# Transposing normalised rows through the vector engine and DRAM instead of the tensor engine, in one fused transformer block

## The chip, the cores and the metric

The kernel runs on one core of a Trainium2 chip. A core has five engines with queues of their own: PE (TensorE, matmuls), DVE (VectorE), ACT (ScalarE), POOL (GpSimd) and SP (SyncE, which here only issues DMAs). Each engine works its queue strictly in order, and engines wait for each other by semaphores. The metric is device time in microseconds (us), the median of several executions.

## What is computed

One pre-norm transformer block in float32, for 4 inputs ("batches", B) of 512 rows (T) by 512 columns (D). Cut to what matters:

```python
x = x + attn(layernorm(x))        # x: (4, 512, 512)
x = x + ffn(layernorm(x))

def attn(n):                      # 32 query heads, 8 key/value heads, 16 wide
    q, k, v = n @ Wq, n @ Wk, n @ Wv
    q, k = rope(q), rope(k)
    p = softmax(causal(q @ k.T / 4))
    return (p @ v) @ Wo

def ffn(n):                       # hidden width 1376
    return (silu(n @ Wg.T) * (n @ Wu.T)) @ Wd.T
```

PE contracts over the partition axis, so each `layernorm(x) @ W` needs the normalised rows transposed: columns of x on the 128 partitions. There are eight such operands of 512 x 512: one ahead of the projections and one ahead of the ffn, for each of 4 inputs.

## The kernel before

Rows are worked in NT = 4 tiles of 128 rows. For one tile, `statistics` (L179) takes mean and variance on DVE and the power of -0.5 on POOL, and `normalised` (L189) writes the normalised rows on DVE. `transposed` (L211) then transposes the tile on PE: four `nc.tensor.transpose` of 128 x 128 against the identity (L214) into one PSUM bank, which ACT (L219) or, for odd tiles outside the first slot, DVE (L217) copies into `xnT`, an SBUF tile of 128 x (4 x 512).

Attention is done in 32 groups, 8 for each input; one group is four heads of one input. `slot(b, steps)` (L673) runs the eight groups of input b by hand in program order. A group has four "visits" (scores on PE at L456 and L461, the row maximum on DVE at L479, the exponential on ACT at L529, the causal mask on POOL at L533), a last visit, and the product with the values (L555). PE work of other stages is handed to a slot as a list of (cost, step) and is spread evenly over it: after each of the 4 visits, `gap()` issues the next steps until the sum of their costs has reached its 32nd part of the whole list. This filling is what keeps PE busy. The lists:

- slot 0 (attention of input 0): projections of inputs 1 (rest), 2 and 3. `projections(b)` gives `begin` (loads of the rows, and statistics and normalisation pushed on a queue), `turned` (the four transposes) and `rest` (24 steps: keys, first queries, values, three more queries, 4 steps each).
- slot 1 (attention of input 1): what is left of input 3's projections, the output product `attended(0)` of input 0 (8 steps, L354) with its normalisation and transposes (`behind`), `hidden(0)` (gate and up products, 44 steps, L399) and half of `down(0)` (20 steps in all, L424).
- slots 2 and 3: the rest of the previous input's `down`, woven with `attended` by `woven` (L722), then `hidden`, then the first half of `down`.
- after slot 3 there is no attention left: the rest of `down` of input 2, then `attended`, `hidden` and `down` of input 3.

DVE work that isn't urgent waits in Python queues. `aside` holds statistics, normalisations and the spread of keys; `full` holds what has to be done with a finished PSUM bank in slot 0; `later` holds the reciprocals of the softmax sums. After each visit, `odd_steps(us)` (L201) takes steps from these queues by their stated costs until a budget of 1.4 to 1.9 is used, so that this work is placed on DVE between one visit's maxima and the next's. Outside slot 0, `fill` also does up to two `aside` steps after each PE step.

The keys' `finish` (L282) rotates the projected keys (DVE shuffle L248, POOL product L249, DVE product L250, POOL sum L251) into `kr` and puts `spread` at the head of `aside`: a DVE shuffle of `kr` (L288) and four POOL products (L290).

A row minimum for each group takes a path through DRAM: `turned_round` (L516, a DVE transpose in 32 x 32 squares, and its store L517) and `laid_out` (L526, four small loads into the next-but-one group's queries). All these DMAs, the loads of rows (L176, L272), of ffn weights (`load_f`, L160) and the stores of results (L429) are issued on SP in program order.

Gate and up weights go through `shared`, three places of 1024 columns; its first two hold Wq and its third Wk and Wv until the projections are done. `load_f(c)` fills place c % 3. `xnTs[""]` is the operand of inputs 0, 2 and 3 and of every ffn; input 1 uses part of `wd_sb`.

The order of slot 1 is, in full:

```python
slot(1, [before[0], *rest3[-12:-4], *before[1:], *rest3[-4:], firsts, *behind,
         *layer[:4], after(spilled), *layer[4:20], after(load_down), *layer[20:], *tiles[:cut]])
```

## Time and profile before

The time is 944.59 us (median of 3 runs, 943.49 to 946.97). The profile shows one execution, whose own time was 946.11 us and whose span (first to last recorded instruction) is 944.4 us.

| | busy us | share of the span | instructions |
|---|---|---|---|
| PE, matmul | 908.7 | 96% | 4672 |
| PE, weight load (beside the matmuls) | 406.3 | 43% | 4672 |
| DVE | 511.8 | 54% | 1514 |
| ACT | 225.0 | 24% | 295 |
| POOL | 216.6 | 23% | 324 |
| DMA, queue of SP | 15.1% of 16 engines | | 64160 packets |

The group boundaries can be read from the first score matmul of each group: slot 0 runs from 60.3 to 204.9 us, slots 1 to 3 from there to about 792 us, and the rest is the tail. Busy time is a share of a stage; where PE is busy without gaps, only less PE work makes the stage shorter, and where it has gaps, what ends the gaps counts.

### The profile page before, as it was taken

What the parts mean: (1) busy time and instruction counts of PE and PEld (TensorE: products, weight loads), DVE (VectorE), ACT (ScalarE), POOL (GpSimd) and SP (SyncE); (2) the same over time, 40 slices, a digit from 0 to 9 for tenths busy, and PEclk for the clock granted to TensorE, in tenths of its full rate; (3) what the DMA queues carried; (4) which work ended last, traced back from release to release, by engine and by line L of the source; (5) the groups of instructions that cost most, each with busy time, mean ns of one, the idle gap of its engine ahead of it and who ended that gap; (6) DMA issues with size and microseconds to landing.
All of it is one profiled execution on the core that took longest, in us unless ns stands there. A gap on an engine that the chain in (4) does not pass through costs nothing.

```text
span 944.4 us, 12662 instructions
## 1 busy us (share of the span) xinstructions
PE 908.7 (96%) x4672; PEld 406.3 (43%) x4672; DVE 511.8 (54%) x1514; ACT 225.0 (24%) x295; POOL 216.6 (23%) x324
## 2 busy tenths in 40 slices
PE   6889889989999999999999999999999999999998
PEld 3444444444444444444444444444444444444443
DVE  7667777767755555565646463666465512422200
ACT  1013333331323232222232322223232321001000
POOL 4554354544221212122111111221111111100000
PEclk9999899999999999999999999999999999999999
DMA  6010100000421610130221110101121011032100
GB/s 222 2 47 2 47 3 2 3 2 2 160 83 41 188 41 24 47 146 12 57 69 45 41 47 13 57 12 47 48 56 46 19 45 67 12 97 72 37 12 33
DMA packets 64510, 47.42 MB, mean 50 GB/s; under 512 B 13536, under 2 KB 56544, under 8 KB 64192
## 3 DMA queue, kind: packets, MB, share of 16 engines
q1 hardware_dynamic: 64160, 40.84, 15.1%
q10 hardware_dynamic: 288, 5.77, 1.6%
q8 instruction: 37, 0.61, 0.3%
q14 instruction: 25, 0.20, 0.1%
HBM read 39.00 MB, written 7.60 MB: 49 GB/s over the span
## 4 chain that ended last, share of the span: by engine, by line
PE 80%; DVE 9%; POOL 5%; issue 2%; ACT 2%; DMA 0%; POOLq 0%; SPq 0%; DVEq 0%; ACTq 0%
PE mm L399 33%; PE mm L424 17%; PE sc L456 13%; PE mm L354 6%; PE sc L461 5%; DVE junk L479 5%; PE mm L240 4%; POOL qa L444 2%; ACT e L529 2%; POOL e L533 1%; PE mm L214 1%; PE av L555 1%; DVE st L183 1%; POOL rot L249 1%; PE mm L303 1%
## 5 line engine op out<-in xcount | busy, mean ns | idle before, releaser
L479 DVE CUSTOM_DVE_ANT_0 junk<-sc,mask 128x128 f32<-128x128 f32 (+3 forms) x512 | 251.1, 490 | 178.0 <-PE sc L461 94.3
L399 PE MATMUL mm<-xnT,shared 128*128 128x512 f32 (+1 forms) x704 | 317.5, 600 | 0.0
L529 ACT ACTIVATE e<-sc 128x1024 f32<-128x1024 f32 (+1 forms) x192 | 165.4, 881 | 477.4 <-PE sc L461 382.5
L399 PEld LDWEIGHTS mm<-xnT,shared 128*128 128x128 f32 (+1 forms) x704 | 127.4, 187 | 166.9 <-issue 161.7
L533 POOL TENSOR_SCALAR_AFFINE_SELECT e<-e 128x512 f32<-128x512 f32 (+1 forms) x160 | 85.2, 543 | 411.9 <-ACT e L529 394.3
L456 PE MATMUL sc<-home,qa 32*128 32x512 f32 (+3 forms) x1024 | 164.7, 464 | 15.3 <-DVE low L479 13.1
L461 PE MATMUL sc<-qa,home 32*128 32x512 f32 (+3 forms) x1024 | 165.9, 472 | 0.5 <-DVE low L479 0.3
L424 PE MATMUL mm<-wd_sb,home 128*128 128x512 f32 (+1 forms) x352 | 158.4, 599 | 0.0
L456 PEld LDWEIGHTS sc<-home,qa 32*128 32x128 f32 x1024 | 76.2, 189 | 116.8 <-issue 30.5
L424 PEld LDWEIGHTS mm<-wd_sb,home 128*128 128x128 f32 (+1 forms) x352 | 64.8, 190 | 83.9 <-issue 82.4
L461 PEld LDWEIGHTS sc<-qa,home 32*128 32x128 f32 x1024 | 72.6, 186 | 26.7 <-issue 14.4
L555 PE MATMUL av<-e,home 128*32 128x512 f32 (+3 forms) x1024 | 78.1, 437 | 0.8 <-POOL e L533 0.7
L408 DVE SCALAR_TENSOR_TENSOR g<-g,mm 128x512 f32<-128x512 f32 (+1 forms) x44 | 29.8, 678 | 81.3 <-ACT g L407 81.3
L240 PE MATMUL mm<-xnT,shared 128*128 128x512 f32 x120 | 62.4, 651 | 1.5 <-issue 0.8
L410 DVE TENSOR_TENSOR home<-mm,g 128x512 f32<-128x512 f32 (+1 forms) x44 | 30.2, 685 | 55.4 <-PE mm L399 55.0
L581 DVE RECIPROCAL inv<-inv 128x128 f32<-128x128 f32 x64 | 58.0, 932 | 0.5
L354 PE MATMUL mm<-wo_sb,cx 128*128 128x512 f32 x128 | 58.1, 600 | 0.0
L407 ACT ACTIVATE g<-mm 128x512 f32<-128x512 f32 (+1 forms) x44 | 26.3, 597 | 116.0 <-PE mm L399 116.0
L555 PEld LDWEIGHTS av<-e,home 128*32 128x32 f32 x1024 | 29.9, 109 | 44.2 <-issue 40.0
L428 DVE SCALAR_TENSOR_TENSOR xr<-mm,xr 128x512 f32<-128x512 f32 x16 | 10.9, 683 | 68.2 <-PE mm L424 68.2
L479 DVE DVE_READ_ACCUMULATOR2_ANT low<- 128x1 f32 x512 | 42.5, 83 | 0.0
L186 POOL TENSOR_TENSOR rstd<-rstd,neghalf 128x1 f32<-128x1 f32 x32 | 21.5, 673 | 73.1 <-DVE rstd L185 73.1
(66 smaller groups left out, 439.0 us busy)
## 6 DMA issues: line engine op xcount, KB each, us to landing
shared<-in_wg SPq DMA_DIRECT2D x40, 256.0 KB
shared<-in_wu SPq DMA_DIRECT2D x40, 256.0 KB
xr<-in_x SPq DMA_DIRECT2D x16, 256.0 KB
out<-xr SPq DMA_DIRECT2D x16, 256.0 KB
xa<-in_x SPq DMA_DIRECT2D x12, 256.0 KB
spill<-wd_sb ACTq DMA_DIRECT2D x1, 2816.0 KB
home<-spill ACTq DMA_DIRECT2D x1, 2816.0 KB
wd_sb<-in_wd SPq DMA_DIRECT2D x1, 2560.0 KB
```

What stands on the lines that cost most here:

```text
L240: nc.tensor.matmul(ps, lhsT=w[:, k, ts(m, P)], rhs=xnT[:, k, :], start=k == 0, stop=k == NK - 1)
L354: nc.tensor.matmul(ps, lhsT=cx[m][:, ts(i, P)], rhs=wo_sb[:, m, :], start=m == 0, stop=m == 3)
L399: nc.tensor.matmul(ps[:m, :], lhsT=wgu[c][:, a, k, :m], rhs=xnTs[""][:, k, :], start=k == 0, stop=k == NK - 1)
L410: nc.vector.tensor_tensor(homes[n][:m, f, :], ps[:m, :], gs[f][:m, :], ALU.mult)
L424: nc.tensor.matmul(py[i], lhsT=homes[n][:m, f, ts(i, P)], rhs=wd_sb[:m, f, :], start=f == 0, stop=f == NF - 1)
L456: nc.tensor.matmul(dst, lhsT=qa[g][rows_of(r), ts(i, P)], rhs=k, start=True, stop=True)
L461: nc.tensor.matmul(dst, lhsT=k, rhs=qa[g][rows_of(r), P * j :], start=True, stop=True)
L479: nc.vector.tensor_tensor_reduce(out=junk[:, :n], in0=src, in1=mask[:, T - n :], scale=-1.0, scalar=BIG, op0=ALU.add, op1=ALU.min, accum_o ...
L529: nc.scalar.activation(dst, src, AF.Exp, scale=1.0 / math.sqrt(DH))
L533: nc.gpsimd.affine_select(out=e[:, heads, c : c + P], in_=e[:, heads, c : c + P], compare_op=ALU.is_ge, fill=0.0, base=0, pattern=[[0, hea ...
L555: nc.tensor.matmul(av[32 * r : 32 * r + 32, P * j :], lhsT=v[:, j, 4 * (m // 2) + r, DH * (1 - hf) : DH * (3 - hf)], rhs=e[:, r, c : c + n ...
L581: nc.vector.reciprocal(r[:, ts(n, P)], r[:, ts(n, P)])
```

## The change

Six of the eight operands (the projections of inputs 2 and 3 and all four of the ffn) are no longer transposed on PE. A new function transposes a normalised tile on DVE in 32 x 32 squares, stores it square by square to its transposed place in a DRAM buffer `flip`, and loads finished column blocks back as `xnT`. Inputs 0 and 1 keep the path over PE. The costs stated for a normalisation in the queue become 1.2 in place of 0.6, those of `turned` and `behind` become 0. Input 3 gets an operand buffer of its own. `spread` of the keys goes to a new queue `soon`, and reaches `aside` at the second `odd_steps` after it. Four steps (input 3's values) move from slot 0 to slot 1, four steps of `down(2)` from slot 3 to the tail, and in `woven` the first four other steps come ahead of `before[0]`. The places of the ffn weights are rotated by two, and the second of the first two weight loads is issued after the last projection step.

```diff
-    xnTs = {"": const.tile([P, NK, T], F32, name="xnT")}
-    xnTs[1] = homes[3][:, :NK, :]
+    xnTs = [const.tile([P, NK, T], F32, name=f"xnT{n}") for n in range(2)]
+    xnT_of = {0: xnTs[0], 1: homes[3][:, :NK, :], 2: xnTs[0], 3: xnTs[1]}
+    flip = [dram.tile([D, T], F32, name=f"flip{n}") for n in range(2)]
...
     def odd_steps(us, banks=True):
+        for n in range(len(soon)):
+            left, step = soon.popleft()
+            if left > 0:
+                soon.append((left - 1, step))
+            else:
+                aside.appendleft(step)
...
+    def flipped(xn, i, n, dst):
+        t = work.tile([P, D], F32, tag="g", name="xt", bufs=2)
+        nc.vector.transpose(t, xn)
+        turned = flip[n].rearrange("(c d) (i r s) -> i r d c s", d=32, r=4, s=32)
+        for r in range(4):
+            rows = t[32 * r : 32 * r + 32, :]
+            nc.sync.dma_start(out=turned[i, r], in_=rows.rearrange("d (c s) -> d c s", s=32))
+        for a in [i - 1, i] if i == NT - 1 else [i - 1] if i > 0 else []:
+            nc.sync.dma_start(out=dst[:, :, ts(a, P)], in_=flip[n].rearrange("(k p) t -> p k t", p=P)[:, :, ts(a, P)])
...
     def norm(i):                                   # in projections
         normalised(xn[i], found[i])
+            if b > 1:
+                flipped(xn[i], i, b % 2, xnT)
...
-                    aside.appendleft((0.75, spread))
+                    soon.append((1, (0.75, spread)))
...
     def norm(i):                                   # in attended
         normalised(xn[i], found[i])
+            flipped(xn[i], i, b % 2, xnTs[0])
...
-        def tail(i):
-            while i not in xn:
+        def tail():
+            while NT - 1 not in xn:
                 do(aside)
-            transposed(xn[i], i, xnTs[""])
...
-        t = shared[:, c % 3, :, :, :]
+        t = shared[:, (c + 2) % 3, :, :, :]
...
-        return [before[0], *others[:4], *before[1:], *others[4:-1], *behind, others[-1]]
+        return [*others[:4], *before, *others[4:-1], *behind, others[-1]]
...
-    slot(0, [begin2, *rest1[8:], *turned2, begin3, *rest2, *turned3, *rest3[:-12]])
+    slot(0, [begin2, *rest1[8:], *turned2, begin3, *rest2, *turned3, *rest3[:-16]])
...
             before[0],
-            *rest3[-12:-4],
+            *rest3[-16:-8],
             *before[1:],
-            *rest3[-4:],
-            firsts,
+            after(lambda: load_f(0)),
+            *rest3[-8:-1],
             *behind,
+            rest3[-1],
+            after(lambda: load_f(1)),
             *layer[:4],
...
     tiles, others = list(down(2, 2)), tiles[cut:]
+    cut -= 4
```

## The prediction, made before the changed kernel was run

> **What bounds the kernel now.** I read first the page's slices of the span, then windows by stage, then what PE waits for in slot 0. In the slices each digit is a tenth of busy time in a 40th of the span.

> ```profile
> PE   6889889989999999999999999999999999999998
> DVE  7667777767755555565646463666465512422200
> ```

> PE is full from slice 9 on (about 206 us); before, it isn't, and DVE is at its busiest there. The windows say the same by stage: the four middle groups of slot 0 and their sum over all eight, then two windows of later stages (after the length: busy time and count for each engine; then PE clock, DMA share, GB/s).

> ```profile
> 115.68:136.16 20.48, 17.02 (x123) 8.63 (x123) 15.41 (x52) 6.34 (x8) 12.44 (x16) 0.92 0.01 3
> 136.16:152.03 15.87, 15.05 (x122) 7.44 (x122) 13.01 (x39) 5.66 (x7) 4.79 (x8) 1.00 0.02 3
> 152.03:167.99 15.96, 15.03 (x110) 6.33 (x110) 10.56 (x40) 6.33 (x8) 8.37 (x10) 1.00 0.01 3
> 167.99:184.64 16.65, 15.23 (x123) 7.37 (x123) 14.58 (x45) 7.12 (x10) 7.36 (x10) 1.00 0.02 3
> ...
> sum 144.64, PE 128.13 PEld 63.12 DVE 107.84 ACT 51.49 POOL 74.20; mean PE 16.02 PEld 7.89 DVE 13.48 ACT 6.44 POOL 9.27
> ```
> ```profile
> 230.60:256.00 25.40, 25.11 (x147) 11.82 (x146) 18.99 (x58) 9.13 (x12) 7.44 (x10) 1.00 0.31 92
> ...
> 795.00:827.00 32.00, 31.76 (x86) 14.79 (x86) 13.82 (x27) 1.17 (x2) 4.34 (x6) 1.00 0.02 9
> ```

> From 206 to 827 us such windows add up to 619.0 of 621 us of PE: there, time is PE work and nothing else. Slot 0 (144.6 us) is mixed. Five of its groups take 15.9 to 17.8 us and three take 20.3 to 20.7. The waits of slot 0 (total, times, longest) and the order of time in a long group say why:

> ```profile
> PE sc L456 <- DVE low L479: 12.2, 11, 3.3
> ...
> DVE ks L288 <- POOL kr L251: 6.5, 3, 2.2
> ```
> ```profile
> 121.86 0.59 PE L456 MATMUL sc<-home,qa 32*128 32x384 f32 x2
> ...
> 124.89 0.01 DVE L288 LOAD_MASK_SELECT ks<-kr  x1 [2.17 <-POOL kr L251]
> ...
> 127.38 1.01 PE L456 MATMUL sc<-home,qa 32*128 32x384 f32 x2 [3.32 <-DVE low L479]
> ```

> DVE stands 2.17 us at the keys' shuffle until POOL has summed `kr`; the row maxima queue behind it, PE's next scores behind those (3.32 us idle), and then the same matmul takes 1.01 us in place of 0.59: PE's clock was lowered. The group at 184.6 has the same (2.63 us idle). The third long group, at 94.9, holds input 2's transposes: PE waits 1.72 us for a PSUM bank that DVE has to empty, then 0.68 us for ACT's copy, and its clock falls to 0.61 from 104 to 112.

> [...] no 512-wide one is in this trace, only L516 with 32 columns (0.211 us). [...] the trace shows SP waiting for the `lowest` store 31 times, 43.0 us in all. [...]

> **The change part by part.** Sums are made against the profiled execution (span 944.4, own time 946.1); the median is 944.6, and I take differences off it.

> 1. ffn operands, 16 tiles. In the tail's order of time, the 16 transposes of one operand hold PE from 822.30 to 824.61:

> ```profile
> 822.30 1.04 PE L214 MATMUL mm<-ident,xn 128*128 128x128 f32 x8
> ...
> 823.57 1.20 PE L214 MATMUL mm<-ident,xn 128*128 128x128 f32 x8 [0.24 <-ACT xnT L219]
> ```

> 2.31 us, 2.4 at 441 and 242, so 4 x 2.35 = 9.4 us gone, all on the path since PE has no gaps there. DVE there loses 8 copies of 0.69 (L217) and gains 16 square transposes, beside a DVE busy about 55%: nothing, except in the chain of step 4.

> 2. Operands of inputs 2 and 3 in slot 0: 32 transposes of about 0.145 us, 4.6 us of PE, and input 2's stall: that group is 4.4 us longer than the clean mean (16.80, 15.87, 15.96, 16.65: 16.3). I take 4 for the stall. Moving input 3's values takes 4.1 us of PE (two runs of L303 x16, 2.05 each) to slot 1, where it costs the same 4.1. DVE gets 8 square transposes. The nearest row is the shuffle L248, 128 x 512, 728 ns; below, the normalisation L191 (0.54); above, 16 x 0.211 = 3.4 if each square pays the start again. [...] I take 0.72: 5.8 us.

> 3. The keys' shuffle. Three waits, of which the long groups show 4.2 and 4.0 us over the clean mean and the first group 1.4 us of PE idle: 9.5. The shuffle now comes two `odd_steps` (some 6 us) later, when POOL's two 1.27 us products are done, so the wait is gone; its 0.72 us and POOL's four products remain. I take 8 of 9.5. Nobody needs these keys before the next slots. What is late next: PE's slot falls to 128.1 - 4.6 - 4.1 less about 5 of clock loss, DVE's rises to 107.8 + 5.8 = 113.6. They are even, so gaps of one show in the other. DVE's share in the fullest clean group is 14.58 / 16.65 = 88%; 113.6 / 0.88 = 129. So I add 4.5 for it. Slot 0: 144.6 - 4.6 - 4.1 - 4 - 8 + 4.5 = 128.4, a gain of 16.2 (6 at 82%, the share of the group at 136; 28 if it reaches 116).

> 4. The way through DRAM. For the size of stores I use DMA of 59.3 to 60.9 us, which holds only one 16 KB store in 128 B packets and one small load, and SP's issues:

> ```profile
> DMA packets 144, 0.02 MB, mean 10 GB/s; under 512 B 144, under 2 KB 144, under 8 KB 144
> ...
> q1 hardware_dynamic: 144, 0.02, 6.8%
> ```
> ```profile
> 59.34 0.34 SPq L517 DMA_DIRECT2D lowest<-turned  x1
> 60.89 2.22 SPq L526 DMA_DIRECT2D qa<-lowest  x4
> ```

> 6.8% of 16 engines x 1.6 us over 144 packets is 12 ns each; the store has landed 1.2 us after its issue, since the load behind it starts then. A tile's four stores are 2048 packets of 128 B, 32 for each engine and store, 0.4 us. Issues of 512-packet DMAs take 0.37 us (L160). So four issues and a landing: 4 x 0.37 + 1.6 = 3.1 us. The load back: 0.37 + 1.2 + 32 packets of 512 B at 27.6 ns (92 GB/s at 31%) = 2.5 us. After the last output product: DVE adds, measures tile 3, normalises and turns tiles 2 and 3, 0.5 + 0.7 + 1.0 + 2 x 1.26 = 4.7. Together 10.3 us until the ffn may start. What covers it: slots 2 and 3, from 428.3 to 451.4 less the transposes, 20.5 us; the tail 14.2 - 2.4 + four moved steps of 7.7 = 19.5; slot 1 eight projection steps, of which four took 4.9 (237.2 to 242.1), so about 10. Slot 1 may stall: 1 us taken, 0 to 6. In slot 0 the stores of a tile precede the third next tile's use of the same one of two `xt` by 6.5 us: enough. Input 2's last normalisation comes near 82 us (79 now, one visit later by the higher cost); with 0.7, `laid_out`'s 2.2 on SP, 3.1 and 2.5 its operand is there near 91. Its keys follow 16 of 48 steps, a third of 128 us after 60.3, near 103: no wait.

> SP: 16 issues and 4 loads for an operand; the last load holds SP about 2 us for its store, with `laid_out` behind it, whose rows are wanted a group (15 us or more) later: nothing. `xr` loads issued four steps later, `load_f` places, the four steps moved to the tail: PE work of the same size where PE is the bound, nothing.

> Sum: -9.4 - 16.2 + 4.1 + 1 = -20.5, so 944.6 becomes 924.

> **The rivals.**
> - *DVE takes over slot 0* (17%): its share stays at 82%, slot 0 gains 6. For it: every visit's maxima wait behind a fuller queue. Against: the group at 168. 944.6 - 9.4 - 6 + 4.1 + 1 = 934.
> - *The stores are serial* (13%, slower): if each of a tile's four stores, whose addresses interleave, has to wait for the one before, a tile takes 4 x (0.37 + 1.6) = 7.9 us, two tiles at the end 15.8. Then slot 1 stalls 11, slots 2 and 3 1 each, the tail 2, and in slot 0 DVE itself stands at `xt` for some 5.6 us an input, 11; with about 2 us of low clock at four places 35 us: 944.6 - 20.5 - 1 + 35 = 958. It decides from about 6.5 us a tile. Against: before, interleaved writes of one `xnT` by two engines overlap (no order was put between them), though that is SBUF:

> ```profile
> 243.60 0.68 DVE L217 COPY xnT<-mm 128x512 f32<-128x512 f32 x1
> ...
> 243.93 0.58 ACT L219 COPY xnT<-mm 128x512 f32<-128x512 f32 x1 [0.75 <-PE mm L214]
> ```

> - *A square transpose costs 3.4 us* (4%): DVE gets 21 us more in slot 0 and the chain 5 in slot 1: 952.

> **How the numbers follow.** The likeliest case has 66%, its own range 912 (slot 0 at 116) to 932 (slot 1 stalls 6, slot 0 at 131). To hold 8 in 10 the range takes in the first rival with its upper edge: 910 to 940. Within 0.5% (4.7 us; less than that can't be told from no change here) lies the upper edge of the first rival and a half-serial second: 5%. Faster 81%, slower 14%.

> **What would show it.** L288 without a wait on POOL; slot 0 near 128 us with three long groups gone and DVE near 88%; L214 down from 128 to 32; one L399 wait of a few us at most, in slot 1, on the load of `xnT`. I am wrong if PE waits at L399 for over 5 us in several slots, if SP waits between the stores of one tile, if the 128 x 512 transpose is far from 0.72 us, or if DVE stands before it.

## The result, and the profile after

The changed kernel takes 940.9 us (median of 11 runs, 939.27 to 941.78), the kernel before in the same comparison 944.59 us (median of 11, 940.55 to 948.82). The ratio is 0.9962, with a 95% interval of 0.9941 to 0.9983: faster by 3.6 us (1.6 to 5.6), where 20.5 were forecast. The forecast of 924.0 is missed, and the time lies 0.9 us above the upper edge of its range. The kernel before varies with PE's clock: in the three later sets of runs 33 of its 112 executions took 940.4 to 941.5 us, about what the changed kernel takes, at a mean granted clock (share of full speed) of 0.997 or 0.998, and the others, like the profiled one (946.11), 942.5 to 949.1 at 0.987 to 0.995. The profiled execution after has a span of 939.2 us, 5.2 less than before.

The table sets the profiled stages beside each other. Here a slot ends with the DVE transpose of row minima (L516 before, L537 after) that closes its last group; slot 3 has no such transpose, and ends where PE starts its last product with the values (L555, L576).

| stage | before, us | after, us | difference | on record |
|---|---|---|---|---|
| opening | 59.1 | 59.5 | +0.4 | 0 |
| slot 0 | 146.2 | 134.8 | -11.3 | -16.2 |
| slot 1 | 192.1 | 202.4 | +10.3 | 4.1 + 1 - 2.35 = +2.75 |
| slot 2 | 200.8 | 199.1 | -1.7 | -2.35 |
| slot 3 | 191.7 | 181.6 | -10.1 | -2.35 and four moved steps, -7.7 |
| tail | 154.6 | 161.7 | +7.1 | -2.35 + 7.7 = +5.35 |

So 4.9 us are missing in slot 0, 7.6 in slot 1, 1.8 in the tail, and under 1 in each other stage. Part of slot 0's difference is clock: in the profiled kernel before, PE ran at half clock there for 13.7 us, in three stretches (from 103.5, 127.4 and 192.2 us), and after for none of it. PE was busy for 13.0 of these 13.7 us, so I estimate their price at half of that, 6.5 us. First the slices of the span after, which answer to those shown of before:

```profile
PE   6888889899799999999999999999999999999998
...
DVE  7668997778455555475647463686564504322200
...
PEclk9999999999899999999999999999999999999999
```

PE's digits reach 9 from slice 8 on, but slice 10 (235 to 258 us), which was full before, now has a hole, and so has the clock. DVE reads 8 to 9 in slices 3 to 5, where it read 7.

Four of the groups of slot 0 after, between first scores as in the prediction, and the sum over all eight (columns as there):

```profile
111.06:128.37 17.31, 14.19 (x108) 5.89 (x109) 16.56 (x49) 6.34 (x8) 9.62 (x12) 1.00 0.33 58
128.37:145.10 16.73, 14.99 (x133) 8.48 (x133) 15.70 (x49) 5.66 (x7) 10.34 (x14) 1.00 0.32 71
145.10:160.44 15.34, 14.24 (x108) 5.95 (x108) 10.10 (x38) 6.33 (x8) 6.56 (x9) 1.00 0.02 3
160.44:178.68 18.24, 14.77 (x109) 6.00 (x109) 16.12 (x50) 5.18 (x6) 9.76 (x12) 1.00 0.02 4
...
sum 133.31, PE 115.63 PEld 52.30 DVE 110.48 ACT 47.03 POOL 69.34; mean PE 14.45 PEld 6.54 DVE 13.81 ACT 5.88 POOL 8.67
```

The three groups of over 20 us are gone and the clock is 1.00 in all of these. But PE, with 12.5 us less work than before, still leaves 17.7 of 133.3 us idle. In the first and second line DVE is busy for 16.56 of 17.31 and 15.70 of 16.73 us, more than PE; over the whole slot its share is 83%, not 88%. What PE waits for in this slot after (total, times, longest):

```profile
PE sc L477 <- DVE low L500: 13.9, 18, 1.9
PE sc L482 <- DVE low L500: 1.7, 4, 0.9
PE av L576 <- POOL e L554: 1.6, 1, 1.6
```

Before, the first of these was 12.2 us in 11 waits, the longest 3.3. The few long waits for row maxima have become many short ones. DVE's wait for the rotated keys (6.5 us in 3) is in no list of after.

The square transpose by shapes, after (busy us, mean ns, idle before it):

```profile
L231 DVE STREAM_TRANSPOSE xt<-xn 128x512 f32<-128x512 f32 x16 | 11.4, 711 | 0.6
L231 DVE STREAM_TRANSPOSE xt<-xa 128x512 f32<-128x512 f32 x8 | 5.7, 711 | 0.3
```

0.711 us was estimated as 0.72, and DVE hardly stands before it.

From slot 1 to the end, PE's waits before come to 1.0 us, all for ACT's copies behind the transposes:

```profile
PE mm L214 <- ACT xnT L219: 1.0, 4, 0.2
```

After, in the whole time from 194 us on, they are:

```profile
PE mm L420 <- DMA xnT<-flip: 5.4, 1, 5.4
PE mm L376 <- POOL cx L605: 2.4, 2, 1.5
PE sc L477 <- DVE low L500: 0.6, 1, 0.6
PE sc L477 <- POOL qa L465: 0.2, 1, 0.2
```

Only one of the four ffn operands is late, that of slot 1. The order of time there (start, duration, engine, line; in brackets the idle time and what ended it):

```profile
227.84 0.69 DVE L379 TENSOR_TENSOR xr<-mm,xr 128x512 f32<-128x512 f32 x1 [0.35 <-PE mm L376]
...
230.89 1.93 SPq L235 DMA_DIRECT2D flip<-xt  x4
...
231.33 0.71 DVE L231 STREAM_TRANSPOSE xt<-xn 128x512 f32<-128x512 f32 x1
...
232.94 0.45 SPq L237 DMA_DIRECT2D xnT<-flip  x1
...
233.42 0.52 SPq L159 DMA_DIRECT2D shared<-in_wg  x1
...
233.99 0.51 SPq L159 DMA_DIRECT2D shared<-in_wu  x1
...
234.60 2.38 SPq L235 DMA_DIRECT2D flip<-xt  x4
...
237.02 2.89 SPq L237 DMA_DIRECT2D xnT<-flip  x2
...
242.61 5.83 PE L420 MATMUL mm<-xnT,shared 128*128 128x512 f32 x8 [5.39 <-DMA xnT<-flip]
```

The last tile has been turned at 232.04, but its stores start at 234.60: SP first issues the stores and a load of other tiles and two loads of weights. Then four issues take 2.4 us. When the operand is there, its first eight matmuls take 5.83 us at a granted clock of 0.63, where eight at full clock take 3.60 to 3.70 in the other runs: the gap has cost 5.4 us and the low clock behind it 2.1 more.

### The profile page after: what moved, and what is told of

Its sections match the earlier page's. It is cut to its first block, busy times and chain, and to the rows that moved or that the text cites. A ratio compares the mean times of both kernels' runs of the same rounds, so it can differ in the third digit from the quotient of the medians.

```text
span 939.2 us, 12679 instructions
## 1 busy us (share of the span) xinstructions
PE 894.3 (95%) x4576; PEld 392.5 (42%) x4576; DVE 521.9 (56%) x1530; ACT 216.4 (23%) x279; POOL 217.4 (23%) x324
## 4 chain that ended last, share of the span: by engine, by line
PE 76%; DVE 13%; POOL 4%; issue 3%; DMA 2%; ACT 2%; SPq 0%; POOLq 0%; DVEq 0%
PE mm L420 34%; PE mm L445 16%; PE sc L477 12%; DVE junk L500 6%; PE mm L376 5%; PE sc L482 4%; PE mm L258 3%; POOL qa L465 2%; ACT e L550 2%; POOL e L554 1%; DVE st L182 1%; DVE inv L602 1%; DVE xa L190 1%; DVE xt L231 1%; PE av L576 1%
## 5 line engine op out<-in xcount | busy, mean ns | idle before, releaser
L420 PE MATMUL mm<-xnT,shared 128*128 128x512 f32 (+1 forms) x704 | 320.0, 604 | 5.4 <-DMA xnT<-flip 5.4
L420 PEld LDWEIGHTS mm<-xnT,shared 128*128 128x128 f32 (+1 forms) x704 | 128.0, 188 | 175.0 <-issue 168.8
L477 PE MATMUL sc<-home,qa 32*128 32x512 f32 (+3 forms) x1024 | 162.3, 459 | 17.8 <-DVE low L500 15.5
L482 PE MATMUL sc<-qa,home 32*128 32x512 f32 (+3 forms) x1024 | 163.6, 467 | 1.8 <-DVE low L500 1.7
L482 PEld LDWEIGHTS sc<-qa,home 32*128 32x128 f32 x1024 | 71.3, 183 | 31.5 <-issue 14.8
L576 PE MATMUL av<-e,home 128*32 128x512 f32 (+3 forms) x1024 | 77.6, 437 | 1.6 <-POOL e L554 1.6
L258 PE MATMUL mm<-xnT,shared 128*128 128x512 f32 x120 | 60.9, 635 | 0.8 <-issue 0.8
L576 PEld LDWEIGHTS av<-e,home 128*32 128x32 f32 x1024 | 29.7, 109 | 44.7 <-issue 39.7
L605 POOL TENSOR_TENSOR cx<-cx,inv 128x256 f32<-128x256 f32 x32 | 23.2, 725 | 77.3 <-DVE inv L602 77.1
```

The lines of the kernel that those rows point to most:

```text
L258: nc.tensor.matmul(ps, lhsT=w[:, k, ts(m, P)], rhs=xnT[:, k, :], start=k == 0, stop=k == NK - 1)
L420: nc.tensor.matmul(ps[:m, :], lhsT=wgu[c][:, a, k, :m], rhs=xnTs[0][:, k, :], start=k == 0, stop=k == NK - 1)
L477: nc.tensor.matmul(dst, lhsT=qa[g][rows_of(r), ts(i, P)], rhs=k, start=True, stop=True)
L482: nc.tensor.matmul(dst, lhsT=k, rhs=qa[g][rows_of(r), P * j :], start=True, stop=True)
L576: nc.tensor.matmul(av[32 * r : 32 * r + 32, P * j :], lhsT=v[:, j, 4 * (m // 2) + r, DH * (1 - hf) : DH * (3 - hf)], rhs=e[:, r, c : c + n ...
```

## The experiments

Times are medians, each ratio is to the kernel before in the same comparison, and differences in us are taken off medians unless a stage is named. Two theories stand for slot 0. *DVE's time*: the slot is as long as DVE makes it, and PE's saved work gains nothing. *Unevenness*: DVE's added work is dear because it comes in a bunch.

### The keys' spread alone

In the kernel before, only the queue `soon` of the change:

```diff
-                    aside.appendleft((0.75, spread))
+                    soon.append((1, (0.75, spread)))
```

> The kernel before with one edit: the keys' spread goes through the queue soon, as in the changed kernel. Theory P (the price of the prediction): the three waits of L288 on POOL go, and with them about 8 us of slot 0: slot 0 near 137 us, time near 936. Theory U (DVE work is uneven between the groups, so a wait that goes is partly taken over by the next DVE queue): 3 to 5 us, time 939 to 942.

944.48 us against 944.03; ratio 1.0011, interval 0.9996 to 1.0026. No gain, where both theories had one. DVE's wait for the rotated keys falls from 6.5 us to 2.2, yet slot 0 is only 0.5 us shorter. The order of time of this run shows where it went:

```profile
127.33 1.52 POOL L299 TENSOR_SCALAR home<-kr,rope_sb 128x512 f32<-128x512 f32 x2
...
128.82 1.52 POOL L299 TENSOR_SCALAR home<-ks,rope_sb 128x512 f32<-128x512 f32 x2
...
130.31 1.26 POOL L258 TENSOR_TENSOR rot<-rot,rope_sb 128x512 f32<-128x512 f32 x1
...
131.66 1.26 POOL L260 TENSOR_TENSOR home<-home,rot 128x512 f32<-128x512 f32 x1
132.87 0.77 POOL L542 TENSOR_SCALAR_AFFINE_SELECT e<-e 128x256 f32<-128x256 f32 x2
...
133.33 0.98 PE L564 MATMUL av<-e,home 128*32 128x256 f32 x8 [3.55 <-POOL e L542]
```

The shuffle no longer stands, but POOL's products for keys and queries now lie ahead of the causal mask of a last visit, and PE's product with the values waits for that mask. PE's waits for the mask come to 4.3 us in this slot, where before they were 0.7. If this is the cause, one visit more of delay helps:

```diff
-                    soon.append((1, (0.75, spread)))
+                    soon.append((2, (0.75, spread)))
```

> The kernel before with the keys' spread put through soon and a delay of 2, so that it reaches DVE and POOL one visit later than in the run with a delay of 1. Theory: in that run the gain was lost because POOL's four spread products stood ahead of the last visit's mask (PE waited 3.55 us for it at 133 us); a visit later they stand ahead of no mask that PE is waiting for, the waits for the rotated keys and for the mask are both gone in slot 0, and the time is 3 to 6 us under the kernel before (938.5 to 941). Rival: the wait only moves again, to the next group's maxima or mask, because DVE and POOL have this work to do in a group that is full anyway; within 1.5 us of the kernel before.

942.14 us against 946.08; ratio 0.9969, interval 0.9953 to 0.9986: 3.9 us by medians and 2.9 by the ratio, at the lower edge of the theory's 3 to 6. PE's longest wait for the mask falls from 3.5 us to 0.7, and the group of input 2's keys from 20.2 us to 17.0. The theory holds in the main, but for two of three waits only; that of input 3 stays, since every queue is emptied ahead of a slot's last group and its keys finish just then:

```profile
185.83 0.01 DVE L297 LOAD_MASK_SELECT ks<-kr  x1 [2.17 <-POOL kr L260]
...
187.92 0.70 PE L465 MATMUL sc<-home,qa 32*128 32x512 f32 x2 [2.63 <-DVE low L488]
```

In the changed kernel, the opposite edit, the spread put back at the head of `aside`:

> The changed kernel with only the spread put back at the head of aside. P: slot 0 longer by about 8 us (near 141, time near 949). U: by 3 to 5 us (near 137, time near 945).

947.46 us; ratio 1.0034, interval 1.002 to 1.0048, so slower than before. Against the changed kernel that is 6.6 us by medians; in the profiles slot 0 is 141.0 us against 134.8. That lies between the two theories; the granted clock is 0.85 in the first group of this slot 0 and 0.91 in the last, some 10.2 us at half clock, against 1.00 throughout in the changed kernel's. The same edit is worth over 6 us here, and 3 to 4 or nothing in the kernel before. That it depends on what stands beside it on POOL was my reading, and was not tested by itself.

### Inputs 2 and 3 back on PE, the ffn as changed

```diff
         def norm(i):                                # in projections
-            if b > 1:
-                flipped(xn[i], i, b % 2, xnT)
...
-            if b < 2:
-                transposed(xn[i], i, xnT)
+            transposed(xn[i], i, xnT)
```

with the costs of before for these steps.

> The changed kernel with inputs 2 and 3 transposed on PE again (costs as before), the four ffn operands still by DVE and DRAM. P: PE gets 4.6 us back and input 2's stall of about 4, DVE is relieved of 5.7 of which 4.5 counted: slot 0 longer by about 4 (near 137, time near 945). U: the groups that normalise are bound by DVE (over 90% busy), so taking 5.7 us of DVE out of them makes up for the PE work: slot 0 within 2 us of 133, time within 3 of 941.

937.37 us; ratio 0.993, interval 0.9905 to 0.9955, and 3.5 us under the changed kernel by medians; slot 0 takes 131.4 us against 134.8. So slot 0 is not longer, as P had it, but shorter, by a little more than U allowed. In slot 0, DVE and DRAM in place of PE lose time. Two runs ask why. One spreads DVE's work, with `begin3` issued eight steps of `rest2` later:

```diff
-    slot(0, [begin2, *rest1[8:], *turned2, begin3, *rest2, *turned3, *rest3[:-16]])
+    slot(0, [begin2, *rest1[8:], *turned2, *rest2[:8], begin3, *rest2[8:], *turned3, *rest3[:-16]])
```

> The changed kernel with one edit: input 3's loads, statistics, normalisation and square transposes start 8 steps (about a group and a half) later in slot 0. Theory U (the groups that normalise are bound by DVE, others have DVE idle, so the same DVE work costs less where it is spread): slot 0 2 to 4 us shorter, time near 938. Rival (it costs the same wherever it stands, because each square transpose delays the next maxima): slot 0 within 1 us of 133 to 135, time within 1.5 us of 941.

939.61 us; ratio 0.9959, interval 0.9938 to 0.9979; slot 0 takes 134.5 us against 134.8. *Unevenness* is not borne out: this placing gains nothing. But it moves the bunch more than it dissolves it, since DVE is busy for over 90% of four of the eight groups, as in the changed kernel, so an even spread stays untried. The other leaves the transposes on PE and gives DVE the square transposes of inputs 2 and 3 as well; nothing reads these:

```diff
+            if b > 1:
+                nc.vector.transpose(work.tile([P, D], F32, tag="g", name="xt", bufs=2), xn[i])
```

> The run with inputs 2 and 3 on PE (937.4) plus one 128x512 square transpose on DVE after each of their eight normalisations, at the changed kernel's stated cost of 1.2; what it writes is not used, and nothing goes to DRAM for it. This adds 5.7 us of DVE work to slot 0, and neither takes PE work away nor adds a transfer. Theory (what slot 0 loses with the new way is DVE time in groups where PE waits for row maxima): slot 0 is 4 to 6 us longer than the 131.4 of that run, time 941 to 943. Rival (the loss comes from the way through DRAM, its issues on SP and its loads): under 1.5 us longer, time 937 to 939.

940.32 us; ratio 0.9959, interval 0.9943 to 0.9976: 2.9 us over the run without them by medians, between the two expectations and nearer to the theory's. Slot 0 shows it more clearly. The sums over its eight groups: inputs 2 and 3 on PE; the same with the unused transposes; the changed kernel.

```profile
sum 131.44, PE 119.12 PEld 56.09 DVE 106.76 ACT 51.15 POOL 70.37; mean PE 14.89 PEld 7.01 DVE 13.35 ACT 6.39 POOL 8.80
```
```profile
sum 134.72, PE 119.92 PEld 56.10 DVE 111.79 ACT 51.15 POOL 70.58; mean PE 14.99 PEld 7.01 DVE 13.97 ACT 6.39 POOL 8.82
```
```profile
sum 134.83, PE 117.15 PEld 52.80 DVE 111.96 ACT 47.03 POOL 69.84; mean PE 14.64 PEld 6.60 DVE 14.00 ACT 5.88 POOL 8.73
```

From the first to the second, 5.0 us of DVE make the slot 3.3 longer. From the second to the third, 2.8 us of PE (4.6 had been priced) and 4.1 us of ACT go and the way through DRAM comes, and the slot stays as long as it was. PE's waits in slot 0 of the second, to be set beside those of the changed kernel shown above:

```profile
PE sc L476 <- DVE low L499: 7.8, 10, 1.7
PE sc L481 <- DVE low L499: 5.0, 4, 1.7
```

PE's waits for row maxima are 12.8 us here and 15.6 in the changed kernel: the 2.8 us of work taken from PE have become 2.8 us of waiting for DVE, and none of PE's waits in slot 0 of the changed kernel is for a DMA. So DVE's time sets this price, the transposes taken from PE were free there, and no cost of the way through DRAM shows. Where the DVE work falls does matter: between the first two runs the second group, where DVE was busy for 70%, grew by 0.3 us for 1.3 more of DVE, and the fourth, at 92%, by 1.5 for 1.8.

### Slot 1: more cover, or an earlier load

First, four more of input 3's projection steps go behind the output product, so that twelve steps cover the way through DRAM in place of eight:

```diff
-            *rest3[-16:-8],
+            *rest3[-16:-12],
...
-            *rest3[-8:-1],
+            *rest3[-12:-1],
```

> The changed kernel with slot 1 reordered only: four projection steps (input 3's queries 1) move from ahead of the output product to behind it, so 11 steps and not 7 stand between the last output product and the ffn. Theory C (PE waits in slot 1 because the cover is shorter than the way through DRAM): the wait of 5.4 us at the first L420 and the half-clock matmuls after it go, 6 to 9 us, time near 933. Theory N (that time comes from elsewhere, the wait only shows it): time within 2 us of 941.

936.99 us; ratio 0.9924, interval 0.9899 to 0.9948; 3.9 us under the changed kernel by medians, less than theory C's 6 to 9, and slot 1 is 5.8 us shorter in the profile. The two differ because the granted clock in this execution's slot 0 is 0.96, against 1.00 in the changed kernel's, and this slot, which the edit doesn't touch, is 3.2 us longer, and because PE now waits 2.0 us for `cx` at the output product where it waited about 1. Second, the two weight loads go ahead of the output product, out of the way of the last stores:

```diff
-            *before[1:],
             after(lambda: load_f(0)),
+            *before[1:],
```

> The changed kernel with one edit: the first ffn weight load stands ahead of the output product in slot 1, not between its last tile's statistics and its last tile's stores. Theory Q (SP's order and the 512 KB of weights in front of the last stores make the way through DRAM longer): the wait at the first L420 falls from 5.4 to 2 to 3.5 us, and part of the half-clock run after it goes: 3 to 5 us, time near 937. Theory R (the way is long by itself: issue, landing, load): the wait stays above 4.5, time within 1.5 us of 941.

939.73 us; ratio 0.9945, interval 0.9924 to 0.9965. The stores of the last tile start at 233.40 in place of 234.60, and the matmuls 1.9 us earlier. The wait falls as theory Q has it, but the time as theory R has it: the gain of 1.2 us by medians is within what runs differ. The first gate product in the two runs, in this order:

```profile
240.48 3.67 PE L420 MATMUL mm<-xnT,shared 128*128 128x512 f32 x8 [0.70 <-DMA xnT<-flip]
```
```profile
240.67 6.50 PE L420 MATMUL mm<-xnT,shared 128*128 128x512 f32 x8 [3.47 <-issue]
```

With cover the gap and the low clock are both gone (0.7 us, and a granted clock of 1.00 over the matmuls); with a gap cut from 5.4 to 3.5 us the clock is still low (0.56), and the eight matmuls take 6.50.

### Together, and what the ffn operands are worth

Inputs 2 and 3 on PE and twelve covering steps:

> The changed kernel with inputs 2 and 3 on PE (as e3) and the longer cover in slot 1 (as e4). If the two causes are separate they add: 3.5 + 3.9 = 7.4 us off 940.9, time near 933.5. If e3 helped only because it shifted slot 1's wait, less than 5 together.

930.53 us; ratio 0.9853, interval 0.9823 to 0.9883; 10.4 us under the changed kernel, 3.0 more than the sum of 7.4. So the two causes are separate; the profiled executions of the two single runs had a mean granted clock of 0.993 and 0.994, and this one 0.999. In the profiles slot 0 gives 3.6 us, slot 1 gives 5.6, and the opening 1.6. To it, the earlier load, and in the tail the pending reciprocals first:

```diff
-    for cost, step in [*woven(before, tiles[cut:], behind), *hidden(3, 0), *down(3, 0)]:
+    for cost, step in [after(lambda: do(later, len(later))), *woven(before, tiles[cut:], behind), *hidden(3, 0), *down(3, 0)]:
```

> As e6, and the first ffn weight load early (as e5), and the reciprocals of the last group put on DVE ahead of the tail's first step, where the store of a down tile stood before them. The wait of PE on POOL's product at the tail's output product (1.5 us in the changed kernel's trace) and the last 0.7 us at the first L420 go: 1.5 to 2.5 us under e6.

929.7 us; ratio 0.9839, interval 0.9812 to 0.9865: the fastest, 11.2 us under the changed kernel by medians. Its step over the run before is 0.8 us, under what was expected; the two waits aimed at are gone, but this execution's opening ends 2.3 us later (60.2 against 57.9). From 194 us on PE waits only here:

```profile
PE mm L373 <- POOL cx L602: 2.0, 1, 2.0
PE sc L474 <- DVE low L497: 0.6, 1, 0.6
```

Last, this kernel with the ffn operands on PE too, so that no operand goes through DRAM:

```diff
         def norm(i):                                # in attended
-            flipped(xn[i], i, b % 2, xnTs[0])
...
-        def tail():
-            while NT - 1 not in xn:
+        def tail(i):
+            while i not in xn:
                 do(aside)
+            transposed(xn[i], i, xnTs[0])
```

> The fastest run so far (929.7) with the four ffn operands transposed on PE again, so that nothing goes through DRAM; its order of steps, its queue for the keys' spread and its early load of weights stay. Theory (where PE is full, PE's work is the time): 4 x 2.35 us more, 938.5 to 940. Rival (the order of steps alone made that run fast, and the transposes were hidden or their place has gaps): under 934.

938.37 us; ratio 0.9932, interval 0.9906 to 0.9959: 8.7 us slower than with the ffn on the new way.

This run says one thing more. No operand goes through DRAM in it, and it still takes 2.5 us less than the changed kernel, of which the reciprocals put first (the wait of 1.5 us in the tail) can explain about 1.5. So the changed kernel owes its gain over the kernel before to its new order of steps. Its transposes, as built, brought nothing: about 9 us saved where PE is full, against some 3.4 lost in slot 0 and 7.5 in slot 1.

## Why the prediction was wrong

The mechanism was right in three of its parts, and two terms were wrong enough to take most of the gain.

- *ffn operands (9.4).* Right: 8.7 between the last two runs, once slot 1 covers the way through DRAM.
- *The square transpose (0.72, my estimate beside the shuffle's 0.728), the stores.* Right: 0.711. The stores of one tile follow each other with no wait between them, so the serial rival is out; SP's waits for a stored tile ahead of its load are 8.3 us in 12 all told, the longest 1.5. The rival of a dear transpose is out too (its own sum, 924 + 21 + 5, is 950 and not 952).
- *Operands of inputs 2 and 3 in slot 0.* This is the first step that failed. The record counts -4.6 for PE and +4.5 for DVE, a wash, in one sum. Measured: +3.3 for DVE's work and 0 for PE's, a loss of 3 to 3.5 and most of the 4.9 us missing in slot 0. Having called PE and DVE even, I still gave PE's saving in full; where PE waits for row maxima from DVE, it is worth nothing. The rival "DVE takes over slot 0" names this cause. It put DVE at 82% of the slot and the slot's gain at 6 us; measured are 83% and 11.3.
- *Input 2's stall (4), the keys' wait (8), the moved values (4.1).* Nearly right in sum, 16.1, against this profiled execution: with inputs 2 and 3 on PE, so without the flip, slot 0 is 14.7 us shorter than before. But some 6.5 of that is PE's clock, as estimated above, and an execution at a mean clock of 0.998 (1.9 us lost in 939) cannot have had these stretches; against such a one the term was too large. The stall went there too, so it wasn't the transposes' own. The 8 belong to the whole new order: `soon` alone gave nothing with the change's delay, as POOL's products then stood ahead of a mask. What is late next was asked of DVE and not of POOL.
- *The way through DRAM in slot 1 (10.3 against a cover of 10, stall 1).* The second step that failed. From the last sum of the output product to the first gate product it took 14.8:

| | on record | measured |
|---|---|---|
| DVE: sums, statistics, normalising, turning | 4.7 | 4.2 |
| SP busy with earlier issues | 0 | 2.6 |
| four stores and their landing | 3.1 | 4.9 (234.60 to 239.5) |
| the load | 2.5 | 3.1 |

  The chain was added up as if SP were idle. The two weight loads were in the diff, ahead of the last stores in program order, and cost two issues; a store's issue took 0.49 us (median) where 0.37 was assumed; and tile 2's load, which waits for its own stores, stands between tile 3's stores and its load. The stall had a range of 0 to 6 and came out at 5.4, but the low clock after it (2.1) was priced only in a rival. Together 7.5 in place of 1.
- *The tail.* The four moved steps cost what they saved, except that DVE now does a finish of `down` ahead of the reciprocals, which keep PE waiting for `cx` for 1.5 us (791.81). I costed this reordering at nothing. With the reciprocals first that wait was gone. The remaining 0.3 us isn't traced.

None of the signs set for being wrong appeared as it was set: the wait at the gate product did pass 5 us, but in one slot and not in several. Of the signs for being right, the keys' shuffle without a wait on POOL came, and slot 0 near 128 us with DVE near 88% did not: it took 133.3 at 83%.

One thing stays open: the wait for `cx` of 2.0 us in slot 1 of the fastest kernel, for which no edit was tried. The opening, which ends at 57.5 to 60.2 us in executions of nearly the same code, blurs single profiles by as much as 2.7 us. In the profiles of the kernel before and of the changed one it ends at 59.1 and 59.5, with 3.41 us at half clock in each (from 48.86 and 48.98 us); that the clock also sets the other executions apart was not shown.

## What to carry to other kernels

Where a change both moves work and reorders steps, run the new order without the moved work as well: here it made the whole gain. Moving work from the engine that holds the end to a slack one pays where the first is full (9 us here), and loses where the second feeds it (3 us here): decide by stage, and count a saving on one side only. Add up a chain that passes through a DMA queue in the program order of that queue, with every issue of other work that stands ahead of it (2.6 us of them here), and give it slack, since a gap can be paid twice (here 5.4 us of waiting and 2.1 of low clock behind it). A wait removed by delaying an instruction can come back where its followers now stand first in line, as when DVE's wait for the keys fell from 6.5 us to 2.2 and PE's for POOL's mask rose from 0.7 to 4.3; ask it of each engine that the delayed step uses.

## What the runs showed of the hardware

- The price of a gap on PE did not follow its length. At the first gate product in slot 1, eight 512-wide matmuls took 6.50 us after 3.5 us idle, 5.83 after 5.4, and 3.67 after 0.7; the granted clock over them was 0.56, 0.63 and 1.00. Two more runs, with inputs 2 and 3 on PE, without and with the unused transposes, had nearly the same gap and a different price:

```profile
239.54 6.31 PE L417 MATMUL mm<-xnT,shared 128*128 128x512 f32 x8 [5.18 <-DMA xnT<-flip]
```
```profile
240.24 5.35 PE L419 MATMUL mm<-xnT,shared 128*128 128x512 f32 x8 [5.08 <-DMA xnT<-flip]
```
